# First scores in 32 by 64 tiles of TensorE, and other queues for the first load and the last store, in a two-layer attention kernel

## The chip, the cores and the metric

The kernel runs on one core of a Trainium2 chip. The metric is the time of one execution in device microseconds. Ten runs of the kernel before gave a median of 3922.5 us, from 3919.42 to 3932.22.

## The reference

The input `x` has 8 images of 32 by 32 tokens with 512 channels, all in fp32. Two attention layers follow one another, each on a group norm of its input (32 groups of 16 channels) and each added to its input:

```python
x = x + conv0(_gn(x), w_qkv, w_proj, b_proj)      # 16 heads of 32
x = x + conv1(_gn(x), Wq, Wk, Wv, Wo, pos_w, pos_h)  # 4 heads of 128
# layer 0, for each image and head, over N = 1024 tokens
attn = softmax((q * 32**-0.5) @ k.T); out = attn @ v       # then @ w_proj + b_proj
# layer 1
scores = q @ k / sqrt(128) + relative_logits(q, pos_w, pos_h)
out = softmax(scores) @ v                                   # then @ Wo
```

## The kernel before, in words

Everything is held with channels on the 128 partitions: an image is a block of four chunks (`CC = 4`) of 128 channels by 1024 tokens, two halves of `NB = 512` tokens (`NH = 2`). Eight such blocks rotate (`BLOCKS = 8`). The program is unrolled; no instruction is executed twice.

**Projections.** A product of 512 by 512 weights with a block is done by a scheme of seven half-size products (`seven`) in place of eight. It needs four differences of weight quarters, which `Matrix.add_up` computes once for each matrix (it fetches the weights, makes four differences of 128 x 512 elements, L139, and stores them to DRAM), and four sums of quarters of the block (`forms`, L325 to L328). Each product is cut by `by_columns` (L305) into tiles of 128 rows by 32 columns of TensorE, four of them side by side.

**First attention** (`attention_0`). Its 512 steps run over 8 images, 4 groups of four heads `m`, 2 halves of the queries `h` and 8 tiles of 128 keys `j`. In a step, `front` computes the scores of four heads of 32 channels: four matmuls (L522), one for each 32 partitions of `k` and `q`, into the four PSUM banks of `ps`, which has one buffer. ACT takes the exponential of all 2048 columns (L530) into `e`. In the next step `back` multiplies `e` by `v` in four tiles of 128 rows by 32 columns (L541) into `acc`, and DVE adds `e` up (L552). `finish` and `normalise` divide by the sums.

**Second attention** (`attention_1`, L637 to L660) adds the logits of the positions by a second matmul with `sel`, a pattern of zeros and ones that four DVE casts fill from `ident` (L106). It first runs at 560 us.

**Order.** The steps of the first attention of image b are interleaved by `side_by_side` with all that can be done beside them: the output projection of the image before, its second attention, the loading and projecting of the next image. A scheduler then orders each engine's instructions by the order in which they were written and by when it expects them to be ready, so that the order on an engine can differ from the text's.

**First image.** `load` fetches blocks of 32 channels by 32 tokens (`load_blocks`, L228: 4 DMAs of 64 KB for each of 8 parts, in pieces of 128 bytes, all on SP's queue); DVE turns each block of 32 by 32 (L700), takes statistics (L241, L242), `put_away` stores the turned image to DRAM for the residual (L210), and `group_norm` normalises in place (L267 to L285), with one power on POOL (rstd, L282). The weights of v (`WV0`) are fetched ahead of it on ACT's queue, and their four differences are DVE's first work. Those of q and k follow behind the image on SP's queue.

**Last image.** `after_1` computes the last projection with the residual (`Onto`, L424 and L429); when a part of 128 channels by 512 tokens is done, `put_out` turns it on DVE (L786) into one of three buffers `ot` and issues four DMAs of 64 KB (L789), all on SP.

Of the kernel before, what the change touches and what calls it, by code (L numbers as in the profile page):

```python
# [9 lines left out]
F32 = mybir.dt.float32  # L10
# [7 lines left out]
P = 128  # L18
# [9 lines left out]
def quick_path(  # L28
# [23 lines left out]
    nc = tc.nc  # L52
# [46 lines left out]


    sel = consts.tile([P, IH, IW], F32R, tag="sel", name="sel")
    for u in range(4):
        rows = slice(32 * u, 32 * u + 32)
        eye = ident[rows, rows]
        eye = eye.unsqueeze(2) if u % 2 else eye.unsqueeze(1)
        nc.vector.tensor_copy(sel[rows], eye.to_broadcast([32, IH, IW]))  # L106
    sel = sel.rearrange("p x y -> p (x y)")


    n_checks = B * (CC + H1) * NH  # L110
# [10 lines left out]
    class Matrix:  # L121
# [4 lines left out]
            self.name = name  # L126
            self.w = w.rearrange("(cc p) n -> p cc n", p=P)[:, :, col0 : col0 + NB]

        def add_up(self, engine, queue, store, keep=False):

            t = block(f"prep_{self.name}")
            whole = t[:, : CC // 2, :].rearrange("p a (b n) -> p (a b) n", n=NB)
            sums = t[:, CC // 2 :, :].rearrange("p a (b c n) -> p (a b) c n", c=HC, n=HN)
            queue.dma_start(whole, self.w)
            b11, b12, b21, b22 = [quarter(whole, i) for i in (11, 12, 21, 22)]
            for i, (x, y) in enumerate(
                [(b12, b11), (b22, sums[:, 0]), (b22, b12), (b21, sums[:, 1])]
            ):
                engine.tensor_tensor(sums[:, i], x, y, op=ALU.subtract)  # L139
            d = dram.tile([P, 4, HC, HN], F32, tag="sums", name=f"ws_{self.name}", bufs=8)  # L140
            store.dma_start(d, sums)
            self.t = d
            self.kept = (whole, sums) if keep else None
# [368 lines left out]
    def attention_0(q, k, v, b):  # L512

        steps = [(m, h, j) for m in (0, 2, 1, 3) for h in range(NH) for j in range(NT)]
        state = {}

        def front(m, h, j):
            name = f"0_{b}_{m}_{h}_{j}"
            ps = psum.tile([P, HB, NB], F32, tag="ps", name=f"ps_{name}", bufs=1)
            for r in range(HB):  # L520
                rows = slice(r * D0, (r + 1) * D0)
                nc.tensor.matmul(  # L522
                    ps[:, r, :],
                    k[m][rows, j * P : (j + 1) * P],
                    q[m][rows, h * NB : (h + 1) * NB],
                    start=True,
                    stop=True,
                )
            e = mem.tile([P, HB, NB], F32, tag="e0", name=f"e_{name}", bufs=2)
            nc.scalar.activation(e, ps, AF.Exp, scale=D0 ** -0.5)  # L530
            return e

        def back(m, h, j, e):
            name = f"0_{b}_{m}_{h}_{j}"
            if j == 0:
                state["acc"] = psum.tile([P, NB], F32, tag="acc", name=f"acc_{name}", bufs=1)
                state["first"] = e
            acc = state["acc"]
            for r in range(HB):
                c0 = (m * HB + r) * D0  # L540
                nc.tensor.matmul(  # L541
                    acc[r * D0 : (r + 1) * D0, :],
                    v[:, j, c0 : c0 + D0],
                    e[:, r, :],
                    start=(j == 0),
                    stop=(j == NT - 1),
                )
            if j == 1:
                state["esum"] = mem.tile([P, HB, NB], F32, tag="es0", name=f"es_{name}", bufs=1)
                nc.vector.tensor_add(state["esum"], state["first"], e)  # L550
            elif j > 1:
                nc.vector.tensor_add(state["esum"], state["esum"], e)  # L552
            if j < NT - 1:
                return
            nc.scalar.copy(q[m][:, h * NB : (h + 1) * NB], acc)
            state["ended"] = (m, h, state["esum"])

        def finish(m, h, esum):
            name = f"0_{b}_{m}_{h}"
            su = psum.tile([P, NB], F32, tag="acc", name=f"sums_{name}", bufs=1)  # L560
            for r in range(HB):
                nc.tensor.matmul(  # L562
                    su[r * D0 : (r + 1) * D0, :],
                    ones[:, :D0],
                    esum[:, r, :],
                    start=True,
                    stop=True,
                )
            normalise(q[m][:, h * NB : (h + 1) * NB], su, name)

        pending = None
        for at in steps:
            if "ended" in state:
                finish(*state.pop("ended"))
            e = front(*at)
            if pending is not None:
                back(*pending)
            pending = (*at, e)
            yield 2
        back(*pending)  # L580
        yield 1
        finish(*state.pop("ended"))
# [44 lines left out]
    def attention_1(q, k, v, posT, b):  # L627

        steps = [(h, c, j) for h in range(H1) for c in range(NH) for j in range(NT)]
        state = {}  # L630

        def front(h, c, j):
            name = f"1_{b}_{h}_{c}_{j}"
            ps = bank(f"ps_{name}")
            keys = slice(j * P, (j + 1) * P)
            queries = slice(c * NB, (c + 1) * NB)
            nc.tensor.matmul(ps, k[h][:, keys], q[:, h, queries], start=True, stop=False)  # L637
            nc.tensor.matmul(ps, sel[:, keys], posT[:, h, queries], start=False, stop=True)  # L638
            e = mem.tile([P, NB], F32, tag="e1", name=f"e_{name}", bufs=3)
            nc.scalar.activation(e, ps, AF.Exp, scale=1.0 / math.sqrt(D1))  # L640
            return e

        def back(h, c, j, e):
            name = f"1_{b}_{h}_{c}_{j}"
            if j == 0:
                state["acc"] = bank(f"acc_{name}")
                state["first"] = e
            acc = state["acc"]
            nc.tensor.matmul(  # L649
                acc,  # L650
                v[:, j, h * D1 : (h + 1) * D1],
                e,
                start=(j == 0),
                stop=(j == NT - 1),
            )
            if j == 1:
                state["esum"] = mem.tile([P, NB], F32, tag="es1", name=f"es_{name}", bufs=2)
                nc.vector.tensor_add(state["esum"], state["first"], e)  # L658
            elif j > 1:
                nc.vector.tensor_add(state["esum"], state["esum"], e)  # L660
            if j < NT - 1:
                return
            nc.scalar.copy(q[:, h, c * NB : (c + 1) * NB], acc)
            state["ended"] = (h, c, state["esum"])

        def finish(h, c, esum):
            name = f"1_{b}_{h}_{c}"
            su = bank(f"sums_{name}")
            nc.tensor.matmul(su, ones, esum, start=True, stop=True)
            normalise(q[:, h, c * NB : (c + 1) * NB], su, name)  # L670

        pending = None
        for at in steps:
            e = front(*at)
            ended = state.pop("ended", None)
            if pending is not None:
                back(*pending)
            pending = (*at, e)
            if ended is not None:
                finish(*ended)  # L680
            yield 0
        back(*pending)
        yield 0
        finish(*state.pop("ended"))

    def load(b, st):
# [18 lines left out]
        yield from group_norm(st, xT, f"0_{b}")  # L705
        st["xn"] = forms(x, f"xn0_{b}")
        yield 0

    def before_first(st):

# [64 lines left out]
    def after_1(b, st, hook=None):  # L775
# [5 lines left out]
        for u in range(2):  # L781

            def put_out(n, h):
                m = n * HC + u
                ot = mem.tile([P, NB], F32, tag="row", name=f"ot_{b}_{m}_{h}", bufs=3)
                nc.vector.transpose(ot, xT[m][:, h * NB : (h + 1) * NB])  # L786
                ot = ot.rearrange("p (t i) -> p t i", i=32)
                for a in range(P // 32):
                    nc.sync.dma_start(  # L789
                        by_blocks(of[b, h * NB : (h + 1) * NB, :], m * P + 32 * a),  # L790
                        ot[32 * a : 32 * a + 32],
                    )
# [69 lines left out]
    plan += units(WO)  # L862

    states = [{} for _ in range(B)]
    WV0.add_up(nc.vector, nc.scalar, nc.gpsimd, keep=True)
    run(load(0, states[0]))
    for m in (WQ0, WK0):
        m.add_up(nc.vector, nc.sync, nc.gpsimd, keep=True)
    stream = Stream(plan)

    def other_sums():
        for m in (WP, WQ1, WK1, WV1, WO):
            m.add_up(nc.gpsimd, nc.gpsimd, nc.gpsimd)
            yield 0

    def at_once(do):
# [538 lines left out]
```

## Time and profile before

| what | before |
|---|---|
| median of 10 runs | 3922.5 us |
| the profiled execution | 3920.14 us, span 3918.3 us |
| TensorE clock granted | 0.996 |
| TensorE busy | 3809.1 us (97%) |
| DVE, ACT, POOL busy | 2523.1, 1721.5, 615.5 us |
| scores of the first attention, L522 | 4096 matmul instructions, 590.5 us |
| its exponential, L530 | 512 of 1879 ns |
| DMA moved | 234.18 MB |

In the profile PE is TensorE's matmul and PEld its weight loads, which run beside matmuls. A line such as `PE L522 MATMUL ps<-q,k 32*128 32x512 f32 x8` says: matmuls of line 522, written to `ps` from `q` and `k`, on a tile of 32 rows by 128 columns, with a moving operand of 32 partitions by 512 columns, eight of them. The ends of matmuls are modelled from their starts. `SPq` is SP's queue of issues; a DMA's own time is told under `DMA`. The chain is the work that ended last, followed back from the end.

### The profile page before, as it was taken

How to read it: one execution, taken by the hardware profiler on the slowest of the kernel's cores; microseconds unless marked ns; L12 is line 12 of the kernel's file. 1: busy time of each engine (PE TensorE's matmuls, PEld its weight loads, DVE VectorE, ACT ScalarE, POOL GpSimd, SP SyncE). 2: the span in 40 equal slices, each digit the busy share in tenths (PEclk: the TensorE clock that was granted, in tenths of full speed). 3: DMA queues.
4: the chain of work that ended last, by engine and by line, in shares of the span. 5: the costliest groups of instructions: out<-in, count | busy, mean ns of one | idle time of the engine just before them, and what ended most of it. 6: DMA issues, size and time to landing. Idle time of an engine off the chain costs nothing.

```text
span 3918.3 us, 71583 instructions
## 1 busy us (share of the span) xinstructions
PE 3809.1 (97%) x30338; PEld 1413.0 (36%) x30338; DVE 2523.1 (64%) x2915; ACT 1721.5 (44%) x1761; POOL 615.5 (16%) x396
## 2 busy tenths in 40 slices
PE   6999899999999999999999999999999999999998
PEld 3222244232443324432343323433234332344353
DVE  5777775577746867458664686656865568754544
ACT  1554553444434454344544445344453445643132
POOL 1341001121111210112101121111210112011101
PEclk9999999999999999999999999999999999999999
DMA  6231120133201422023120241103311123110401
GB/s 168 72 110 41 47 60 6 39 115 70 60 2 50 115 62 55 9 90 84 47 54 16 92 93 38 46 23 98 87 44 33 30 91 69 31 63 20 122 17 23
DMA packets 498694, 234.18 MB, mean 60 GB/s; under 512 B 286368, under 2 KB 478144, under 8 KB 497344
## 3 DMA queue, kind: packets, MB, share of 16 engines
q1 hardware_dynamic: 495232, 214.79, 20.5%
q0 software_dynamic: 2608, 13.70, 0.9%
q8 instruction: 241, 3.95, 0.4%
q10 hardware_dynamic: 528, 1.05, 0.1%
q14 instruction: 85, 0.70, 0.1%
HBM read 170.72 MB, written 58.72 MB: 59 GB/s over the span
## 4 chain that ended last, share of the span: by engine, by line
PE 86%; DVE 8%; ACT 3%; issue 2%; POOL 1%; DMA 1%; SPq 0%; DVEq 0%; POOLq 0%; ACTq 0%
PE ps L522 12%; PE ps L637 11%; PE acc L649 11%; PE acc L541 10%; PE y_q L305 4%; PE y_k L305 4%; PE y_v L305 4%; PE ps L638 3%; PE x_v L305 3%; PE z_k L305 3%; PE x_k L305 3%; PE x_q L305 3%; PE z_q L305 3%; PE z_v L305 3%; ACT e L530 2%; DVE es L552 2%
## 5 line engine op out<-in xcount | busy, mean ns | idle before, releaser
L530 ACT ACTIVATE e<-ps 128x2048 f32<-128x2048 f32 x512 | 961.9, 1879 | 842.4 <-PE ps L522 646.9
L552 DVE TENSOR_TENSOR es<-es,e 128x2048 f32<-128x2048 f32 x384 | 888.2, 2313 | 402.9 <-ACT e L530 400.5
L522 PE MATMUL ps<-q,k 32*128 32x512 f32 x4096 | 590.5, 642 | 33.4 <-ACT e L530 33.2
L640 ACT ACTIVATE e<-ps 128x512 f32<-128x512 f32 x512 | 305.7, 597 | 586.5 <-PE ps L638 550.0
L541 PE MATMUL acc<-e,v 128*32 128x512 f32 x4096 | 548.4, 607 | 0.4 <-ACT su L488 0.4
L637 PE MATMUL ps<-q,k 128*128 128x512 f32 x1024 | 523.6, 593 | 0.3 <-DVE posT L623 0.3
L649 PE MATMUL acc<-e,v 128*128 128x512 f32 x1024 | 521.9, 592 | 0.0
L660 DVE TENSOR_TENSOR es<-es,e 128x512 f32<-128x512 f32 x384 | 291.6, 759 | 265.0 <-ACT e L640 263.7
L510 POOL TENSOR_TENSOR q<-q,su 128x512 f32<-128x512 f32 x128 | 214.3, 1674 | 1568.2 <-DVE su L506 1567.4
L638 PE MATMUL ps<-posT,sel 128*128 128x512 f32 x512 | 406.7, 794 | 0.0
L522 PEld LDWEIGHTS ps<-q,k 32*128 32x128 f32 x4096 | 161.5, 183 | 429.2 <-ACT e L530 212.6
L637 PEld LDWEIGHTS ps<-q,k 128*128 128x128 f32 x1024 | 193.6, 190 | 246.1 <-issue 240.6
L649 PEld LDWEIGHTS acc<-e,v 128*128 128x128 f32 x1024 | 193.1, 189 | 146.8 <-issue 105.0
L541 PEld LDWEIGHTS acc<-e,v 128*32 128x32 f32 x4096 | 81.6, 108 | 386.0 <-issue 341.5
L550 DVE TENSOR_TENSOR es<-e,e 128x2048 f32<-128x2048 f32 x64 | 175.1, 2736 | 38.9 <-ACT e L530 38.9
L490 DVE STREAM_TRANSPOSE tu<-su 128x512 f32<-128x512 f32 x128 | 90.7, 708 | 135.9 <-ACT su L488 135.7
L638 PEld LDWEIGHTS ps<-posT,sel 128*128 128x128 f32 x512 | 97.3, 190 | 122.5 <-issue 122.5
L488 ACT COPY su<-sums 128x512 f32<-128x512 f32 x128 | 74.9, 585 | 149.4 <-PE sums L562 81.5
L658 DVE TENSOR_TENSOR es<-e,e 128x512 f32<-128x512 f32 x64 | 44.2, 690 | 145.7 <-ACT e L640 145.7
L623 DVE TENSOR_TENSOR posT<-pp,posT 32x512 fp32r<-32x512 f32 x128 | 111.9, 874 | 31.8 <-ACT posT L618 30.4
L414 POOL TENSOR_TENSOR k<-b_k,p_k 128x512 f32<-128x512 f32 x32 | 50.6, 1582 | 477.2 <-ACT p_k L379 477.2
L618 ACT CAST posT<-pp 32x512 fp32r<-32x512 f32 x128 | 105.6, 825 | 45.1 <-PE pp L605 43.9
(188 smaller groups left out, 4504.5 us busy)
## 6 DMA issues: line engine op xcount, KB each, us to landing
w_qkv<-ws_qkv SPq DMA_DIRECT2D x168, 128.0 KB, 2.4
xs<-in_x SPq DMA_DIRECT2D x256, 64.0 KB, 2.5
d<-x0T SPq DMA_DIRECT2D x32, 512.0 KB, 3.4
x1T<-d SPq DMA_DIRECT2D x32, 512.0 KB, 5.2
d<-x1T SPq DMA_DIRECT2D x32, 512.0 KB, 3.3
x2T<-d SPq DMA_DIRECT2D x32, 512.0 KB, 6.0
out<-ot SPq DMA_DIRECT2D x256, 64.0 KB, 2.0
w_qkv<-in_L_conv_w_qkv SPq DMA_DIRECT2D x126, 128.0 KB, 2.2
```

Source lines behind the costliest of these rows:

```text
L305: ins = nc.tensor.matmul(out[columns, :], weights[:, columns], moving, start=start, stop=stop, skip_group_check=open_sum,)
L510: nc.gpsimd.tensor_tensor(dst, dst, su, op=ALU.mult)
L522: nc.tensor.matmul(ps[:, r, :], k[m][rows, j * P : (j + 1) * P], q[m][rows, h * NB : (h + 1) * NB], start=True, stop=True,)
L530: nc.scalar.activation(e, ps, AF.Exp, scale=D0 ** -0.5)
L541: nc.tensor.matmul(acc[r * D0 : (r + 1) * D0, :], v[:, j, c0 : c0 + D0], e[:, r, :], start=(j == 0), stop=(j == NT - 1),)
L550: nc.vector.tensor_add(state["esum"], state["first"], e)
L552: nc.vector.tensor_add(state["esum"], state["esum"], e)
L637: nc.tensor.matmul(ps, k[h][:, keys], q[:, h, queries], start=True, stop=False)
L638: nc.tensor.matmul(ps, sel[:, keys], posT[:, h, queries], start=False, stop=True)
L640: nc.scalar.activation(e, ps, AF.Exp, scale=1.0 / math.sqrt(D1))
L649: nc.tensor.matmul(acc, v[:, j, h * D1 : (h + 1) * D1], e, start=(j == 0), stop=(j == NT - 1),)
L660: nc.vector.tensor_add(state["esum"], state["esum"], e)
```

## The change

There are four edits.

1. `front` makes the scores of a step with eight matmuls in place of four: the 128 keys of a tile are cut into two halves of 64, so each matmul uses 32 rows by 64 columns of TensorE and writes 64 partitions of its bank.
2. The first image is loaded by `load_first`: eight DMAs of 128 whole rows (256 KB, pieces of 2 KB), in turn on SP's and ACT's queue, into a block `x_rows`. TensorE turns each 128 by 128 piece by a transpose with `ident` into PSUM, ACT and DVE copy the banks out, and six matmuls whose results aren't used follow. Statistics are taken at the end, chunk by chunk. Later images are loaded as before.
3. `add_up` is split into `fetch` and `add_up`. v's weights are fetched on SP right behind the first image's rows, and their differences are POOL's instead of DVE's. `sel` is filled behind the differences of q's and k's weights.
4. For the last image every second output DMA is issued on ACT's queue.

```diff
+        def fetch(self, queue):
+            t = self.t = block(f"prep_{self.name}")
+            whole = t[:, : CC // 2, :].rearrange("p a (b n) -> p (a b) n", n=NB)
+            queue.dma_start(whole, self.w)
...
-            for r in range(HB):
-                rows = slice(r * D0, (r + 1) * D0)
-                nc.tensor.matmul(
-                    ps[:, r, :],
-                    k[m][rows, j * P : (j + 1) * P],
-                    q[m][rows, h * NB : (h + 1) * NB],
-                    start=True,
-                    stop=True,
-                )
+            for i in range(2):
+
+                some = slice(64 * i, 64 * i + 64)
+                for r in range(HB):
+                    rows = slice(r * D0, (r + 1) * D0)
+                    nc.tensor.matmul(
+                        ps[some, r, :],
+                        k[m][rows, j * P + 64 * i : j * P + 64 * i + 64],
+                        q[m][rows, h * NB : (h + 1) * NB],
+                        start=True,
+                        stop=True,
+                    )
...
+    def load_first(st):
+
+        rows = block("x_rows", [P, NT, C])
+        for t in range(NT):
+            queue = nc.scalar if t % 2 else nc.sync
+            queue.dma_start(rows[:, t, :], xf[0, t * P : (t + 1) * P, :])
+        WV0.fetch(nc.sync)
+        x = block("x0T_0")
+        xT = chunks(x)
+        for h in range(NH):
+            if h == 0:
+                whole = psum.tile([P, CC, NB], F32, tag="ps", name="turned_0", bufs=1)
+                banks = [whole[:, cc, :] for cc in range(CC)]
+            else:
+                banks = [bank(f"turned_1_{cc}") for cc in range(CC - 1)]
+                banks.append(psum.tile([P, NB], F32, tag="acc", name="turned_1", bufs=1))
+            for t in range(NT // NH):
+                for cc in range(CC):
+                    nc.tensor.transpose(
+                        banks[cc][:, t * P : (t + 1) * P],
+                        rows[:, h * (NT // NH) + t, cc * P : (cc + 1) * P],
+                        ident,
+                    )
+            for cc in range(CC):
+                part = xT[cc][:, h * NB : (h + 1) * NB]
+                if h == 0 or cc % 2:
+                    nc.scalar.copy(part, banks[cc])
+                else:
+                    nc.vector.tensor_copy(part, banks[cc])
+
+        idle = psum.tile([P, CC, NB], F32, tag="ps", name="idle", bufs=1)
+        for t in range(6):
+            nc.tensor.matmul(idle[:, t % CC, :], ident, rows[:, t, :], start=True, stop=True)
+        for cc in (1, 0, 3, 2):
+            statistics(st, xT, cc, "0_0")
+        st["kept"] = put_away(xT, "0_0")
+        run(group_norm(st, xT, "0_0"))
+        st["xn"] = forms(x, "xn0_0")
...
-                    nc.sync.dma_start(
+
+                    queue = nc.scalar if b == B - 1 and a % 2 else nc.sync
+                    queue.dma_start(
...
-    WV0.add_up(nc.vector, nc.scalar, nc.gpsimd, keep=True)
-    run(load(0, states[0]))
+    load_first(states[0])
+    WV0.add_up(nc.gpsimd, nc.gpsimd, keep=True)
     for m in (WQ0, WK0):
-        m.add_up(nc.vector, nc.sync, nc.gpsimd, keep=True)
+        m.fetch(nc.sync)
+        m.add_up(nc.vector, nc.gpsimd, keep=True)
+    fill_sel()
```

More of the change, by code (lines that the diff above doesn't have):

```diff
@@ L101, in quick_path, with fill_sel @@
     sel = consts.tile([P, IH, IW], F32R, tag="sel", name="sel")
[L102 to L107, printed above, removed]
+    def fill_sel():
+        for u in range(4):
+            rows = slice(32 * u, 32 * u + 32)
+            eye = ident[rows, rows]
+            eye = eye.unsqueeze(2) if u % 2 else eye.unsqueeze(1)
+            nc.vector.tensor_copy(sel[rows], eye.to_broadcast([32, IH, IW]))
+    sel_flat = sel.rearrange("p x y -> p (x y)")
     n_checks = B * (CC + H1) * NH
@@ L127, in __init__, with add_up @@
             self.w = w.rearrange("(cc p) n -> p cc n", p=P)[:, :, col0 : col0 + NB]
-        def add_up(self, engine, queue, store, keep=False):
-            t = block(f"prep_{self.name}")
+        def fetch(self, queue):
+            t = self.t = block(f"prep_{self.name}")
+            whole = t[:, : CC // 2, :].rearrange("p a (b n) -> p (a b) n", n=NB)
+            queue.dma_start(whole, self.w)
+        def add_up(self, engine, store, keep=False):
+            t = self.t
             whole = t[:, : CC // 2, :].rearrange("p a (b n) -> p (a b) n", n=NB)
             sums = t[:, CC // 2 :, :].rearrange("p a (b c n) -> p (a b) c n", c=HC, n=HN)
-            queue.dma_start(whole, self.w)
             b11, b12, b21, b22 = [quarter(whole, i) for i in (11, 12, 21, 22)]
@@ L637, in front @@
             nc.tensor.matmul(ps, k[h][:, keys], q[:, h, queries], start=True, stop=False)
-            nc.tensor.matmul(ps, sel[:, keys], posT[:, h, queries], start=False, stop=True)
+            nc.tensor.matmul(ps, sel_flat[:, keys], posT[:, h, queries], start=False, stop=True)
             e = mem.tile([P, NB], F32, tag="e1", name=f"e_{name}", bufs=3)
@@ L872, in other_sums @@
         for m in (WP, WQ1, WK1, WV1, WO):
-            m.add_up(nc.gpsimd, nc.gpsimd, nc.gpsimd)
+            m.fetch(nc.gpsimd)
+            m.add_up(nc.gpsimd, nc.gpsimd)
             yield 0
```

## The prediction

> **What bounds the kernel now.** I read the page's busy shares and the shares of the chain first, then a table of busy time by stage, cut at the start, the first attention alone, the interleaved middle, and the tail.
>
> ```profile
> PE 3809.1 (97%) x30338; PEld 1413.0 (36%) x30338; DVE 2523.1 (64%) x2915; ACT 1721.5 (44%) x1761; POOL 615.5 (16%) x396
> PE 86%; DVE 8%; ACT 3%; issue 2%; POOL 1%; DMA 1%; SPq 0%; DVEq 0%; POOLq 0%; ACTq 0%
> ```
>
> ```profile
> 0.00:31.20 31.20, 0.00 (x0) 0.00 (x0) 19.84 (x39) 1.28 (x1) 5.31 (x16) 1.00 0.90 211
> ...
> 86.00:560.00 474.00, 448.26 (x4156) 135.94 (x4152) 342.17 (x302) 250.82 (x194) 107.49 (x66) 0.98 0.21 67
> 560.00:3463.00 2903.00, 2879.48 (x23052) 1051.98 (x23048) 1919.10 (x2202) 1333.85 (x1346) 435.25 (x265) 1.00 0.21 57
> ...
> 3906.30:3918.30 12.00, 0.00 (x0) 0.00 (x0) 0.00 (x0) 0.00 (x0) 0.00 (x0) 0.54 0.45 67
> ```
>
> Columns: stretch, length, then busy us (and count) of PE, PEld, DVE, ACT, POOL, last the clock, DMA share and GB/s. Three things are to be seen. From 560 to 3463 us TensorE is busy 99% and DVE 66%: what shortens TensorE's work there shortens the kernel one for one. The first 31.2 us have no matmul. The last 12 us have no engine at work, only output on its way. The change touches these three places.
>
> Next, one step of the first attention in order of time, and the durations (min/median/max, ns) of its two matmul groups from the answers for lines 522 and 541:
>
> ```profile
> 1006.05 1.14 PE L522 MATMUL ps<-q,k 32*128 32x512 f32 x8
> 1007.13 1.06 PE L541 MATMUL acc<-e,v 128*32 128x512 f32 x8
> 1008.01 0.40 PE L305 MATMUL y_v<-w_v,f_xn 128*32 128x256 f32 x4
> ```
>
> ```profile
> L522 PE MATMUL ps<-q,k x24: 587/640/692, 1006.1 to 1015.9; 32*128 32x512 f32 x24
> L541 PE MATMUL acc<-e,v x24: 592/605/617, 1007.1 to 1016.9; 128*32 128x512 f32 x24
> ```
>
> An fp32 matmul is two instructions, so a score step of four matmuls is eight, in two rounds of four tiles. The start of L541 less that of L522 is 1.08 us, against 0.88 us for the equally many instructions of L541, which are followed by the same tile shape. Streaming is 0.43 us a round in both (L541: 0.88 over two). Single records give the rest: in the first round all four L522 matmuls last 692 ns, in the second 587, so 105 ns of the first round is waiting for its own 128 columns of weights; for 32 columns (L541) it is 617 - 592 = 25 ns. The tiles of a round start 6.8 ns after one another. And where the shape changes, the next weight load comes 515 to 521 ns after the **last** start of the round before, whether that round was staggered by 20 ns or not, that is 85 to 91 ns after it has streamed.
>
> **What the Trainium skill says.** TensorEngine Tiling (Tiling Modes) lists 32x64 as eight tiles that work in parallel, and says that a change of mode drains the engine. The trace agrees on the drain (the 85 to 91 ns); tiles cut both by row and by column occur nowhere in it. TensorE: Matmul & The Clock Gate (Part 3, Packing small matmuls) gives 10.6 times for 16 tiles of 32 by 32: evidence that both cuts go together. The same page (LDWEIGHTS) has the load grow with the columns, P/1.2 ns, 53 ns for 64; the line through my 25 and 105 gives 52. DMA: Bandwidth & Descriptors (Issuing engines are not separate DMA queues) says that a second issuing engine saves only issue time. The trace has the 16 DMA engines 70 to 84% busy while one queue issues the last outputs, which fits.
>
> **Part 1, scores on tiles of 32 by 64.** Eight matmuls instead of four in each of 512 steps, 16 weight loads and 16 matmul instructions instead of 8 and 8, each still streaming 512 columns. If eight tiles run at once, streaming stays at two rounds of 0.43 us. Before, the fourth tile's first round streams from 3 x 6.8 + 105 = 125 ns after the step's first load; after, the eighth tile's from 7 x 6.8 + 52 = 100 ns. The switch counts from the last tile, so 25 ns a step: 512 x 25 = **12.8 us**, which I take at 12.5. The second round's loads hide under the 430 ns of the first, as now. The 32 instructions of a step come at about 32 ns each; v's projections, 64 instructions in 1.73 us, show 27 ns sustained, so issue holds. The exponential (L530) waits for the last matmul and gets it 25 ns sooner too, so steps that wait for ACT (the 474 us stage) gain as well. What is late next is TensorE itself; DVE at 66% has room. Best end: without any stagger 105 - 52 = 53 ns, 27 us gained. Worst end inside this case: the two column halves of a row group load one after the other, 48 + 105 = 153 against 125 ns, 14 us lost.
>
> **Part 2, the first batch.** Now 32 loads of 64 KB in 128-byte pieces; DVE turns and measures them as they land, and the chain of waits alternates between `xs<-in_x` and SP's issues (about 0.5 us each) up to 25.45 us:
>
> ```profile
> 25.45 0.72 DVE x0T L700
> 26.19 0.70 DVE st L241
> 26.92 0.22 DVE mv L242
> 27.16 0.22 DVE turned L267
> 28.73 0.26 DVE back L275
> 29.26 1.05 POOL rstd L282
> 30.34 2.99 DVE x0T L285 x4
> ```
>
> After: eight loads of 256 KB, four on SP and four on ACT, in 2 KB pieces. Such pieces took 84 ns on one of 16 DMA engines (v's weights, same stretch), so 1024 of them are 5.4 us; from 2.2 us (first packets) and with some 1.4 us to the semaphore they are in at about 9, and v's 1 MB behind them 2.7 us later, long before use. TensorE turns 32 blocks, two instructions each. The nearest row is a 128x128 matmul of 512 columns at 0.43 us an instruction; for 128 columns that is 0.107, so 0.21 us a block, and double while the clock is low (the first products have 0.43 us a round where later ones have 0.215): 32 blocks take 7 to 14 us from about 4, end 11 to 18, taken 14. Copies out (ACT 0.58, DVE 0.69 us each, four over two engines): 15.5. Eight statistics at 0.74 and four sums at 0.25 are 6.9 us on DVE; if half of them ran before the last blocks, 3.5 remain, otherwise all: 19 to 22.4, taken 21. Then the group norm's chain as above, 30.34 - 27.14 = 3.2 us, and its first chunk 0.87 us: first product at about 25 instead of 31.2, 6 us. Against it: v's four weight sums move to POOL (1.27 us each alone, up to 3.3 beside DVE, ahead of or behind rstd), the six warming matmuls (0.86 us each, at most 10 us on a slow clock, inside the wait for the norm), and the norm in place waits for the four 512 KB stores of x0T (1.3 us each plus 2 to land, about 23 us, inside). I take 1 us: **5 us** gained, between 10 and -2. Moving `sel` costs nothing: 2.8 us of DVE, which is idle until the first data, and if placed later still needed only by the second attention at 560 us. On SP 32 issues (22.9 us) give way to four and v's fetch, which leaves ACT's queue; there four row loads of some 0.5 us stand ahead of a table load and six copies that need the data anyway. The fetches of q's and k's weights stay on SP; if they land late, DVE's eight sums (4.9 us) do too, covered by v's products.
>
> **Part 3, the last outputs.**
>
> ```profile
> 3904.32 1.89 DVE L786 STREAM_TRANSPOSE ot<-x2T 128x512 f32<-128x512 f32 x3
> 3905.05 9.48 SPq L789 DMA_DIRECT2D out<-ot  x12
> ```
>
> Twelve outputs leave after the first of the last three turned tiles, 0.79 us each with two stalls of some 2 us, and 3.8 us follow (landing, flag, end). With six on ACT, issue would need 6 x 0.55 = 3.3 us; but the DMA engines, 80% busy at 0.55 us an output, need 0.44 each, 5.3 us. So 9.5 becomes about 5: **4.5 us** gained, between 7 and 1. On ACT only four copies of the last projection stand behind its issues (0.59 us each); each may come an issue or two later, which TensorE would feel once or twice: inside the range.
>
> Sum: 12.5 + 5 + 4.5 = 22 us. The profiled execution took 3920.14 us (span 3918.3), so 3898; the median of the ten is 3922.5, 2.4 above it, so **3900.5**.
>
> **The rivals.** (a) *Eight tiles don't run at once.* If TensorE takes the 32x64 tiles four at a time, a step has four rounds and not two: 2 x 0.43 = 0.86 us more, 512 times, 440 us: 4345. If only the second half's first round overlaps, 0.43 us: 4125. For it: no row here shows more than four tiles. Against: column tiles already read the same partitions four times over, and the 32x128 rounds write as much PSUM. With 9.5 us from parts 2 and 3, it ends slower by 0.2% once a step grows by (9.5 + 7.8)/512 = 34 ns. (b) *The stagger eats the load.* If each further tile costs 13 ns instead of 6.8, the eighth streams from 143 ns, fronts lose 9 us, and parts 2 and 3 leave about nothing: 3922. (c) *The start gains nothing*, since turning on a slow clock or statistics left in a row at the end take as long as the loads did: parts 1 and 3 alone, 3905. (d) *The change doesn't do what it says*: the wait for weights is not the load's length but a fixed cost of a change of shape; L541's 25 against L522's 105 speaks against it. Then fronts gain nothing or lose the 28 ns of stagger: 3913 to 3927.
>
> **How the numbers follow.** The forecast (c included) 0.71, its own range 3880 to 3914; (b) and (d) 0.14, half of it within 0.2%; (a) 0.15. A measurement of this kernel can tell about 0.2%, 7.8 us, from no change. Faster: 0.71 and a few of (d), 0.73; same 0.10; slower 0.17. The range 3880 to 3928 leaves out (a) and little else.
>
> **What would show it.** Right: L522 with 8192 matmuls of 32*64, first round near 640 ns, weight load to L541's about 1.045 us; first product near 25 us; last output issued near 3892. Wrong: L522's busy time near 1030 us instead of 590, or a first matmul of the step still at 692 ns. If the kernel is above 3930 us, step one of part 1, that eight tiles stream at once, was wrong.

## The result, and the profile after

The kernel after takes 3902.5 us (median of 8 runs, 3897.99 to 3906.6) against 3923.5: a ratio of 0.9945, 95% interval 0.9937 to 0.9954, some 21 us. The profiled execution took 3901.37 us (span 3899.6), 18.8 us less than that of before. The line numbers moved: L522 is now L532, L530 L540, L541 L551, L305 L312, L139 L146, L786 L835, L789 L840.

First the busy shares and two groups of the page:

```profile
PE 3807.3 (98%) x34478; PEld 1371.7 (35%) x34478; DVE 2516.7 (65%) x2905; ACT 1724.1 (44%) x1767; POOL 622.6 (16%) x400
...
L532 PE MATMUL ps<-q,k 32*64 32x512 f32 x8192 | 576.4, 614 | 36.2 <-ACT e L540 36.2
```

Twice as many score matmuls as before have less busy time than before (576.4 against 590.5 us): eight tiles run at once. Next, three rows of the table by stage. The middle begins at 560 us in both tables and ends at the last exponential:

```profile
0.00:26.60 26.60, 10.62 (x44) 6.97 (x45) 15.28 (x33) 4.41 (x7) 11.09 (x21) 0.90 0.96 331
...
560.00:3446.00 2886.00, 2860.14 (x26245) 1014.03 (x26243) 1909.32 (x2185) 1327.43 (x1339) 435.93 (x264) 1.00 0.21 57
...
3890.70:3899.60 8.90, 0.00 (x0) 0.00 (x0) 0.68 (x2) 0.00 (x0) 0.00 (x0) 0.58 0.59 88
```

The stretch ahead of the first product is 26.6 us instead of 31.2. The interleaved middle is 2886 us instead of 2903 at the same 99% of TensorE; since it begins at the same time in both, these 17 us hold what was gained ahead of it too. From the end of the last turned tile to the end of the span it is 8.2 us instead of 12.1 (the last row begins 0.7 us earlier). Then one step, in order of time, and its groups:

```profile
1002.01 1.11 PE L532 MATMUL ps<-q,k 32*64 32x512 f32 x16
1003.05 1.07 PE L551 MATMUL acc<-e,v 128*32 128x512 f32 x8
```

```profile
L532 PE MATMUL ps<-q,k x32: 587/613/638, 1002.0 to 1006.3; 32*64 32x512 f32 x32
```

L551 starts 1.04 us behind L532, before it was 1.08. All eight matmuls of a first round last 638 ns where all four lasted 692, the second round 587 in both. The longest is the first round: 51 ns over the second, for 64 columns of weights.

Where the profiled executions part is seen by laying the same events side by side:

| event | before, us | after, us | difference |
|---|---|---|---|
| first product | 31.21 | 26.62 | -4.6 |
| first exponential | 86.73 | 81.38 | -5.4 |
| 129th step's exponential | 815.08 | 805.80 | -9.3 |
| 449th | 3187.51 | 3172.07 | -15.4 |
| last exponential | 3461.84 | 3446.82 | -15.0 |
| last product | 3902.99 | 3888.70 | -14.3 |
| end of the span | 3918.26 | 3899.58 | -18.7 |

So the start gave 5.4 us, the 512 steps 9.7, the last projection took 0.7 back, and the end gave 4.4. These are single executions: the kernel after was profiled once more (e11), and there the first product came at 26.12 us, the first exponential at 79.48 and the last at 3447.57.

### The profile page after: what moved, and what is told of

Read it like the earlier page. It is cut to its first block, busy times and chain, and to the rows that moved or that the text cites. A ratio compares the mean times of both kernels' runs of the same rounds, so it can differ in the third digit from the quotient of the medians.

```text
span 3899.6 us, 79833 instructions
## 1 busy us (share of the span) xinstructions
PE 3807.3 (98%) x34478; PEld 1371.7 (35%) x34478; DVE 2516.7 (65%) x2905; ACT 1724.1 (44%) x1767; POOL 622.6 (16%) x400
## 4 chain that ended last, share of the span: by engine, by line
PE 85%; DVE 8%; ACT 3%; issue 2%; POOL 1%; DMA 0%; SPq 0%; DVEq 0%; POOLq 0%; ACTq 0%
PE ps L647 11%; PE acc L659 11%; PE ps L532 11%; PE acc L551 10%; PE y_k L312 4%; PE y_v L312 4%; PE y_q L312 4%; PE ps L648 3%; PE x_v L312 3%; PE z_k L312 3%; PE x_k L312 3%; PE x_q L312 3%; PE z_v L312 3%; PE z_q L312 2%; ACT e L540 2%; DVE es L562 2%
## 5 line engine op out<-in xcount | busy, mean ns | idle before, releaser
L540 ACT ACTIVATE e<-ps 128x2048 f32<-128x2048 f32 x512 | 961.6, 1878 | 843.9 <-PE ps L532 602.1
L532 PE MATMUL ps<-q,k 32*64 32x512 f32 x8192 | 576.4, 614 | 36.2 <-ACT e L540 36.2
L551 PE MATMUL acc<-e,v 128*32 128x512 f32 x4096 | 547.6, 606 | 0.4 <-ACT su L495 0.4
L532 PEld LDWEIGHTS ps<-q,k 32*64 32x64 f32 x8192 | 120.2, 130 | 432.3 <-ACT e L540 216.8
L551 PEld LDWEIGHTS acc<-e,v 128*32 128x32 f32 x4096 | 81.5, 108 | 412.7 <-issue 365.2
```

The source lines that it names most:

```text
L532: nc.tensor.matmul(ps[some, r, :], k[m][rows, j * P + 64 * i : j * P + 64 * i + 64], q[m][rows, h * NB : (h + 1) * NB], start=True, stop=True,
L551: nc.tensor.matmul(acc[r * D0 : (r + 1) * D0, :], v[:, j, c0 : c0 + D0], e[:, r, :], start=(j == 0), stop=(j == NT - 1),)
```

## Experiments: one part at a time

In the first four, the kernel before had a median of 3923.9 us.

**e1: only the tiles.** The kernel before, with this in `front`:

```diff
-            for r in range(HB):
+            for i in range(2):
+                some = slice(64 * i, 64 * i + 64)
+                for r in range(HB):
...
-                    k[m][rows, j * P : (j + 1) * P],
+                        k[m][rows, j * P + 64 * i : j * P + 64 * i + 64],
```

> The kernel before with the eight 32x64 score tiles alone. Theory A (weight load less stagger, some given back as waits): step from its weight load to the next shape's 1.044 us against 1.071, 512 times 26 ns is 13 us, of which the trace after shows about 10 between the first and the last exponential: 3913, ratio 0.9973. Theory B (the tiles do nothing and the middle gained by another order of instructions): 3923, ratio 1.000. Theory C (nothing given back): 3910, ratio 0.9966.

Measured: 3915.5 us, 0.998 (0.9973 to 0.9986), 8.4 us less. From a step's first score load to L551's first load (here L544) the median was 1.044 us instead of 1.071. Some 498 of the 512 steps have this interval without another wait in it, in either kernel, and it is 26.6 ns shorter there, 13.6 us for 512 steps. The mechanism is the one forecast; of these 13.6 us, 8.4 arrived.

**e2: only the two ends.** The kernel after, with `front` as it was (32 by 128, four matmuls).

> The kernel after with the scores on four tiles of 32x128 as before: first load and last store alone. Theory A: 5 us at the start and 4.4 at the end, 3914, ratio 0.9976; first exponential about 5.4 us sooner and the same offset at the last. Theory B (the middle's gain comes with the new start): 3904, ratio 0.995. If the start's gain were lost in waits of the first attention: 3919.

Measured: 3912.5 us, 0.9972 (0.9961 to 0.9983), 11.4 us less. With the first exponential its profile is 6.7 us ahead of before, and 6.5 to 5.9 ahead through the middle, so the ends don't make the steps shorter. At 3296 us its lead drops to 4.3, across a stretch of halved TensorE clock that the profile of before doesn't have there (more on this at the end). 8.4 and 11.4 are 19.8, against the 21 of the whole change: the parts add up.

**e3: only the output's second queue.** The kernel before, with

```diff
-                    nc.sync.dma_start(
+                    queue = nc.scalar if b == B - 1 and a % 2 else nc.sync
+                    queue.dma_start(
```

> The kernel before with the last image's outputs on two queues alone. Theory A: issue and transfer of the last outputs overlap, end 4.4 us sooner: 3919, ratio 0.9989. Theory B (the 16 DMA engines are the limit, a second queue brings nothing): 3923.5, ratio 1.000.

Measured: 3921.1 us, 0.9993 (0.9985 to 1.0001), between the two. Its profile shows the gain itself, 12.73 to 9.07 us from the last turned tile to the end, and a cost: from its first `y_wo` product, which ends the last long wait (3.1 us in every profile), to the last product, the last projection took 24.0 us instead of 21.2. Some 1.7 us of that go with a stretch of 3.4 us at half TensorE's clock at 3884 us; e1, without this edit, has such a stretch at 3875 us and took 22.9. The other 1.1 us belong to this edit: e5, e9, e10 and e11, which have it and no such stretch there, took 22.3. The 192 matmuls are the same, but TensorE runs them in another order; how the edit brings that about was not followed. The median alone can't tell 2.7 us from nothing; 3.7 gained less 1.1 lost comes near it.

**e4: 16 tiles of 32 by 32.** The kernel after, with

```diff
-            for i in range(2):
-                some = slice(64 * i, 64 * i + 64)
+            for i in range(4):
+                some = slice(32 * i, 32 * i + 32)
```

> The kernel after with 16 score tiles of 32x32 a step. Theory A (load and stagger): the 16th tile streams from 15 x 6.75 + 25 = 126 ns after the step's first load, against 100 with 64 columns and 125 with 128: 26 ns a step are lost again, first round's matmuls last 612 ns, step 1.07 us, 10 to 13 us slower than after: 3913 to 3916. Theory B (load alone, the stagger doesn't count): 27 ns gained a step, 3889 to 3892. Theory C (issue: 64 instructions a step at 27 ns is 1.73 us): 0.66 us more a step, about 4240.

Measured: 3921.8 us, 0.9996 (0.9988 to 1.0005): some 19 us are lost against the kernel after, and 9.3 against e2, which has the same ends and four tiles. Sixteen tiles are worse than four.

Its scores in two steps (min/median/max ns), and one step in order of time:

```profile
L532 PE MATMUL ps<-q,k x64: 587/598/612, 1002.5 to 1008.6; 32*32 32x512 f32 x64
```

```profile
1008.04 1.16 PE L532 MATMUL ps<-q,k 32*32 32x512 f32 x32
1009.13 1.07 PE L551 MATMUL acc<-e,v 128*32 128x512 f32 x8
```

The load did shrink again (612 ns, 25 over the second round, as the columns say). But the step became longer. In the records of the step shown the first 14 tiles of a round start 6.7 ns apart, up to 88 ns; the last two come at 103 and 120 ns (in 346 of the 512 steps the last starts at about 120; in 39 it is near 152). So what starts last sets the step: 120 + 22 = 142 ns to the last tile's stream, against 7 x 6.7 + 51 = 98 with eight tiles and 3 x 6.8 + 105 = 125 with four. From load to load the medians are 1.087, 1.044 and 1.071 us, and lie as far apart as these sums. With the even stagger of theory A it would have been 126 ns; why the last tiles come late stays open. With issue as the bound it would have been some 4240 us.

## Experiments: what held the first product at 26.6 us

The image's rows had landed by about 10 us and TensorE had turned them by 11.1; the first product came 15 us later. VectorE in that time, in the kernel after:

```profile
14.50 0.19 DVE L249 BATCH_NORM_AGGREGATE mv<-st 128x2 f32<-128x12 f32 x1
16.68 1.69 DVE L146 TENSOR_TENSOR prep_qkv<-prep_qkv 128x512 f32<-128x512 f32 x1 [1.99 <-DMA prep_qkv<-in_L_conv_w_qkv]
18.30 0.20 DVE L249 BATCH_NORM_AGGREGATE mv<-st 128x2 f32<-128x12 f32 x1
18.42 1.82 DVE L248 BATCH_NORM_STATS2 st<-x0T 128x6 f32<-128x512 f32 x3
20.16 0.18 DVE L249 BATCH_NORM_AGGREGATE mv<-st 128x2 f32<-128x12 f32 x1
20.27 0.63 DVE L248 BATCH_NORM_STATS2 st<-x0T 128x6 f32<-128x512 f32 x1
20.82 0.67 DVE L146 TENSOR_TENSOR prep_qkv<-prep_qkv 128x512 f32<-128x512 f32 x1
```

L146 are the differences of q's weights. The scheduler had placed the first of them in the middle of the statistics, and all that follows waited 2 us for the weights' DMA and then for the difference itself, 1.69 us while one of GpSimd's ran. Three more stand ahead of the norm.

**e5 and e10: these differences behind the forms.** The kernel after, with

```diff
+        last_form[0] = nc.vector.tensor_sub(s4, a12, s2)
...
-        m.add_up(nc.vector, nc.gpsimd, keep=True)
+        with tc.issue_after(last_form[0].ins):
+            m.add_up(nc.vector, nc.gpsimd, keep=True)
```

> The changed kernel with the additions that sum the query and key weights put behind the last form of the first batch's queries and keys. In the changed kernel five of them, of some 1.7 us each, stand between the statistics and the forms on VectorE. Theory D (VectorE's queue sets the first product): the first product comes some 3 us earlier, at about 23.5 us instead of 26.6, and the time is about 3 us below the changed kernel's: some 3899, ratio 0.9937 to the kernel before. Rival E (those additions only fill time in which VectorE waits, or their result is late at the projection): first product at 26 to 27 us, or the gain is handed back by the first stage's end; time 3902, ratio 0.9945.

> The version with the late weight sums once more, to compare it with the changed kernel on one chip. If its 3898.3 was no accident of where the half-clock windows fell, it is again 3 to 4.5 us below the changed kernel, ratio 0.9926 to 0.9934; if it was, it is within 1.5 us of it.

Measured: 3898.3 us, 0.9928 (0.9915 to 0.9942); once more, 3899.1 us, 0.9938 (0.9924 to 0.9952). Run beside the first, a version equal to the kernel after but for its unused matmuls (e7) had 3901.8; beside the second, the kernel after itself (e11) had 3903.1: 3.5 and 3.9 us less, with five runs each that spread over 6 to 8 us. The first product came at 21.56 and 21.94 us, earlier still than D said, since without the interruption the statistics ran from 12.02 to 17.4 us. Theory D holds.

**e6, e7, e8: the unused matmuls.** `range(6)` was made `range(18)`, removed, and made `range(14)` together with the edit of e5.

> The changed kernel with 18 matmuls on data that nobody uses in place of 6 between the transposes and the first product, so that TensorE is busy until about 26 us. In the changed kernel TensorE stands from 16.2 to 26.6 us and the first product runs at a granted clock of 0.5 and takes 3.64 us. Theory W (the wait before the first product costs the clock): first product in about 1.9 us and the clock full behind it, the time 2 to 5 us below the changed kernel's: 3897 to 3900, ratio 0.9933 to 0.994. Rival N (VectorE's forms pace the first products, so a faster clock waits for the next form): no difference, 3902, ratio 0.9945.

> The changed kernel without the six matmuls on data that nobody uses. If they have no effect on the clock of the first product, which is half in any case, and lie beside work of VectorE and ScalarE, the time is the changed kernel's, 3902, ratio 0.9945, and the first product comes at 26.6 us as before. If they keep the clock of something that I have not seen, it is 2 to 4 us slower: 3905, ratio 0.9953.

> Both of the above: the weight sums behind the last form, and 14 matmuls on data that nobody uses. If theories D and W both hold, first product at about 23.5 us in 1.9 us, and the time 4 to 7 us below the changed kernel's: 3895 to 3898, ratio 0.9927 to 0.9936. If only D holds 3899, if neither 3902.

Measured: e6 3904.7 us, 0.9949 (0.9936 to 0.9963); e7 3901.8, 0.9941 (0.9927 to 0.9954); e8 3901.4, 0.9941 (0.9928 to 0.9955). TensorE in e6:

```profile
26.45 1.93 PE L312 MATMUL x_v<-prep_qkv,x0T 128*32 128x256 f32 x32
31.26 3.42 PE L312 MATMUL y_v<-prep_qkv,f_xn 128*32 128x256 f32 x32 [2.87 <-DVE f_xn L333]
```

The first products took 1.93 us instead of 3.64, as theory W has it, and then TensorE waited 2.87 us for a form: rival N. The first exponential came at 80.78 us, between the 81.38 and 79.48 of the kernel after's two profiles. In its profile 3.0 us are lost near 210 us, as the next experiment shows; whether that is why e6 is slower in its other runs is not known. e8 missed its forecast: its 14 unused matmuls kept TensorE to 23.79 us, 2.2 us longer than the data needed. Without any (e7) the first product was at 26.91 us and nothing measurable changed, so the six of the change do nothing.

**e9: GpSimd's sums of the other weights on VectorE.** In e5 the first exponential was 6.8 us ahead of the kernel after, the 64th only 3.2. Two views of e5, VectorE and GpSimd over the same stretch, in order of time:

```profile
205.67 6.12 DVE L563 TENSOR_TENSOR es<-es,e 128x2048 f32<-128x2048 f32 x1 [1.47 <-ACT e L541]
211.72 0.68 DVE L381 TENSOR_TENSOR b_k<-y_k,p_k 128x512 f32<-128x512 f32 x1
```

```profile
205.90 3.74 POOL L146 TENSOR_TENSOR prep_v<-prep_v 128x512 f32<-128x512 f32 x3
```

An addition with a median of 2.29 us took 6.12, the length by which it is longer being that of three sums of GpSimd, and the products of k waited 2.3 us for the `b_k` behind it. This is not a trait of e5. The same kernel run once more (e10) has additions of 3.42 and 2.95 us at this place, no such wait, and keeps its lead; and of the kernel after, the second profile (e11) has it where the first has not:

```profile
209.01 6.14 DVE L562 TENSOR_TENSOR es<-es,e 128x2048 f32<-128x2048 f32 x1 [1.47 <-ACT e L540]
215.08 0.68 DVE L380 TENSOR_TENSOR b_k<-y_k,p_k 128x512 f32<-128x512 f32 x1
```

```profile
PE y_k L312 <- DVE b_k L380: 2.3, 1, 2.3
```

So the collision, worth some 3 us, comes in some executions of one kernel and not in others. The edit to e5:

```diff
             m.fetch(nc.gpsimd)
-            m.add_up(nc.gpsimd, nc.gpsimd)
+            m.add_up(nc.vector, nc.gpsimd)
```

> The version with the late weight sums (3898.3), and the twenty weight sums of the other five matrices on VectorE instead of GpSimd. In that version the first product came 5.1 us earlier than in the changed kernel, but only 3.2 us reached the 64th exponential: at 205.7 us one addition of VectorE took 6.12 us instead of 2.3 to 3.1, beside GpSimd's sum of v's weights (3.74 us), and the products of k waited 2.3 us for b_k behind it. Theory L (the two engines hold each other up): without these sums on GpSimd no addition of VectorE is that long, the wait for b_k is gone, and 1 to 3 us come back: 3895.5 to 3897.5, ratio 0.9921 to 0.9926. Rival M (twenty sums of 0.68 us are 14 us more for VectorE in a stage in which it is on the path at times): 3898 to 3903, ratio 0.9928 to 0.994.

> The changed kernel itself, beside the two above: 3902, ratio 0.9945.

Measured: 3893.2 us (3890.7 to 3895.5), 0.9924 (0.9911 to 0.9938), against 3903.1 (3899.2 to 3905.4) for the kernel after and 3899.1 (3893.7 to 3901.3) for e10, run beside it. What a sum costs is in the groups of L146, of e5 and of e9 (min/median/max):

```profile
L146 POOL TENSOR_TENSOR prep_q<-prep_q x4: 1262/3023/3328, 158.1 to 165.9; 128x512 f32<-128x512 f32 x4
```

```profile
L146 DVE TENSOR_TENSOR prep_q<-prep_q x4: 677/679/692, 152.8 to 154.7; 128x512 f32<-128x512 f32 x4
```

On VectorE a sum takes 0.68 us; on GpSimd 1.26 alone and up to 3.3 beside VectorE, and it holds VectorE up in turn. The additions of that stage, of e5 and of e9:

```profile
L563 DVE TENSOR_TENSOR es<-es,e x78: 2239/2293/6122, 84.6 to 542.6; 128x2048 f32<-128x2048 f32 x78
```

```profile
L563 DVE TENSOR_TENSOR es<-es,e x78: 2239/2293/3179, 84.7 to 537.9; 128x2048 f32<-128x2048 f32 x78
```

The longest fell from 6.12 to 3.18 us, the wait for `b_k` is gone, and the 64th exponential was 8.7 us ahead of the kernel after, 2.5 ahead of e10, and the last one 3.0 ahead of e10. Theory L holds. The Trainium skill's page SBUF — State Buffer (SBUF: two separate sides) gives a mechanism that fits the lengths: GpSimd and a VectorE operation with two inputs in SBUF share a pair of ports that one of them locks for a whole instruction. By that page the one that starts first gets the pair; here the record of the addition begins 0.23 us ahead of GpSimd's sums and three of these still went ahead of it, so this part is not shown.

e9 beats both kernels: 30.8 us below the one before, 9.9 below the one after, and its longest run is shorter than the shortest of e11. e10 has an addition of 6.18 us as well, at 163.6 us, and lost nothing by it: whether such a collision reaches TensorE depends on what stands behind it. The 5.9 us between the medians of e10 and e9 are uncertain, since their runs overlap, and how they part into collisions avoided and sums that are simply shorter, no run here separates.

## Why the prediction was right, point by point

Forecast were 3900.5 us and 22 us gained; measured 3902.5 and 21. The range and the likeliest case held. That the sum came so near is in part luck: in the two profiled executions it is 18.8 us, with 9.7 for the tiles where 12.5 were forecast, and in part 2 two errors cancelled.

**Part 1, 12.5 us.** Every step of its mechanism is in the trace: 8192 matmuls, eight at once, 638 ns for the first round (640 forecast), 1.044 us from load to load (1.045), the next load still 515 to 521 ns behind the last start. The intervals are 26.5 ns shorter, 13.6 us for 512. What was mis-sized is the term "512 times", and with it the readings that TensorE's time in the middle counts one for one and that steps which wait for ACT gain as well: only 9.7 us (8.4 in e1) reached the last exponential. In the first 128 steps the lead grows by 31 ns a step (9.27 less 5.36 us), but some 1.7 us of that come from a half-clock stretch at 186.6 us that only the profile of before has (the lead jumps from 5.4 to 7.3 us there), which leaves about 17 ns; from there to the 449th it grows by 19 (15.43 less 9.27, over 320). Part of a saved nanosecond is waited away. From the first to the last exponential TensorE stood for 52.8 us in all instead of 49.3, with 17.1 us at half clock in both: 13.6 less 3.5 is near the 9.7. The longest kinds of these waits in the middle, after and before (line, what it waited for, us in total, times, longest):

```profile
PE ps L532 <- ACT e L540: 14.9, 13, 2.7
PE y_wo L312 <- DVE a_wo L372: 8.9, 7, 1.4
```

```profile
PE ps L522 <- ACT e L530: 13.1, 13, 2.6
PE y_wo L305 <- DVE a_wo L365: 8.6, 7, 1.4
```

2.1 us more in the same 20 waits. That a step which waits for ACT's 1.88 us of exponential is set by ACT would explain it; it was not tried by a run. **Rival (b)**, the stagger, was real but one cut further on: with eight tiles it stays 6.7 ns, with sixteen the last ones come late (e4). **(a)** fell, with eight and with sixteen tiles (its 4345 and 4125 us were mis-added: with its own 440 and 220 us and parts 2 and 3 alone they are 4353 and 4133); **(d)** fell by the 638 and 612 ns.

**Part 2, first product at 25 us, 5 us gained.** 26.62, and 5.4 at the first exponential (26.12 and 7.3 in e11), so rival **(c)** fell. Two errors inside nearly cancelled. TensorE had turned the blocks by 11.08 us, where the prediction took 14, and they were copied out by 12.1, not 15.5: a block is one instruction and not two as the prediction had it from the matmuls, 8 of them in 1.09 us. And of the eight differences of q's and k's weights, which it called covered by v's products, four lay ahead of the norm on VectorE, and so ahead of these products: the step that failed is the sentence on weights that land late. They cost some 5 us of first product (e5), 3.5 to 3.9 of the kernel. What was said of v's sums on GpSimd (12.77 to 17.8 us, done in time) and of `sel` held; the six matmuls are hidden, as said (e7).

**Part 3, 9.5 to 5 us, 4.5 gained.** The two queues' issues, of the kernel after in order of time:

```profile
3888.37 0.71 DVE L835 STREAM_TRANSPOSE ot<-x2T 128x512 f32<-128x512 f32 x1
3889.11 5.22 SPq L840 DMA_DIRECT2D out<-ot  x6
3889.11 5.22 ACTq L840 DMA_DIRECT2D out<-ot  x6
```

9.48 became 5.22 us, near the 5.3 worked out from the DMA engines' share; from the start of the last turned tile to the end, 12.73 became 8.87. ACT's copy at 3880.55 us did stand behind six issues, and the last projection became 1.1 us longer with this edit (see e3). That is the cost of an issue or two which the prediction allowed for, though it came as another order of the products and not as a gap: behind that copy TensorE has none above 0.15 us. So part 3 is worth 3.9 less 1.1 us, 2.8 and not 4.5.

## What to carry to other kernels

Where tiles of another shape follow, price a step by when its last tile begins to stream, tiles times stagger plus the load of its columns: it has a minimum (here eight tiles), and beyond it both more and fewer lose. Write down what each engine's queue holds ahead of the first product: work that could be done later, but was placed where its data were expected, cost some 4 us here, where the unused matmuls brought nothing that could be measured. And keep small elementwise work off GpSimd where VectorE is adding beside it: a sum there took up to five times as long (3.3 us against 0.68), and VectorE's wait came on top.

## What the runs showed of the hardware that I had not expected

TensorE's clock is decided over windows of 3.413 us: in all 13 profiles every stretch at full or at half clock, up to the last one, lasts a whole multiple of it (3.413, 6.827, 68.267 us). Counting TensorE's busy share in each such window, from 45 us on: a full clock was halved for the next window 70 times, behind a window with a busy share of at most 0.46 in 69 of them; it stayed full some 14,400 times, behind 0.40 or more; and a halved clock came back behind 0.83 or more. In the first 45 us this last figure is less sharp: the clock came back behind 0.77 (e4) and stayed halved behind 0.80 (the kernel after). And the kernel after got its full clock at 7.72 us, when TensorE had run nothing but the transposes, from 4.96 us on, so those count as work. The Trainium skill's TensorE: Matmul & The Clock Gate (Part 1) has the window and that it runs free, but asks for a whole idle window; the measurement says that 2 us of waiting within one are enough. So where a wait falls decides whether it costs more than itself: the kernel after waits 2.16 us at 106.5 and has a half-clock window at 110.1 us, and it waits 2.10 us at 177.8, cut by a window's edge, and has none. Such a window costs up to half of itself, 1.7 us, as in e2, whose lead over before falls from 5.9 to 4.3 us across the one at 3296 us. Between 45 and 3878 us the profiles have 6 of them (before and after), 10 in e1 and 4 in e4. Two of e1's four more lie behind its last exponential, and from there to the last product it took 444.7 us instead of 441.2. This count is an argument and not an experiment.
